# The last block's values made among the first attention scores, with the on-chip buffers of two stages laid out anew

## The chip, the cores and the metric

The kernel runs on one core of a Trainium2 chip, as one program. The metric is the time of one execution on the device in microseconds (us), and for several runs their median. The kernel before took 3134.0 us in the median of three runs (3131.89, 3134.0 and 3134.24).

## The reference

4096 nodes with 256 features each pass through two layers, both with the same adjacency matrix `adj`:

1. a graph attention network of two levels (8 heads of width 32; the weights are a softmax of leaky sums over the neighbours);
2. a transformer layer with 8 heads of width 32 and a mask.

The change concerns the second layer:

```python
qkv = layer_norm(x, g1, be1) @ w_qkv
qkv = qkv.reshape(n, 3, HEADS, HEAD_DIM)
q, k, v = (qkv[:, 0], qkv[:, 1], qkv[:, 2])
scores = jnp.einsum('nhd,mhd->hnm', q, k) * SCALE
mask = (adj != 0)[None, :, :]
scores = jnp.where(mask, scores, -jnp.inf)
attn = jax.nn.softmax(scores, axis=-1)
out = jnp.einsum('hnm,mhd->nhd', attn, v).reshape(n, DIM)
x = x + out @ w_proj + b_proj
h2 = layer_norm(x, g2, be2)
ff = jax.nn.gelu(h2 @ w1 + b1) @ w2 + b2
return x + ff
```

## The kernel before

Four stages follow each other on one core: the graph attention network (up to about 1600 us of the profile), the projections to queries, keys and values (to about 1690 us), masked attention (to about 2865 us) and the feed-forward part (to the end). The change touches the second stage and the beginning of the third, both in `unshifted_transformer`. Line numbers are those of the profile.

**The projections (L1782 to L1853).** The nodes are cut into eight blocks of 512 (`nb`). For each block PE does, in this order:

- it turns the normed rows of the next block (`Ahead.turned`, L1598; 8 transposes at L1556), and ScalarE writes them as columns `hn` (L1559);
- four tiles of keys and then queries (`i` is 1 and then 0, `c` is 0 and 1; L1810), each of 128 × 512 in fp32. ScalarE casts a tile to fp16 (L1817), and VectorE takes the rest that the cast lost (L1818). The halves lie in `u_halves`, three buffers, and SP writes them to `half_d` in DRAM (L1822);
- four tiles of values (L1829), which ScalarE copies to `v_sb` (L1836), the tile `u_v` of the profile.

An fp32 matrix multiplication shows as two passes in the profile, so a block has 16 passes at L1810 and 16 at L1829. One pool, `u_ps_q`, gives the eight banks of PSUM in turn to transposes, keys, queries and values.

The keys come back from `half_d` into two tiles `u_k` (`stack`, L1734). Of blocks 0 to 4 only half is loaded, and VectorE copies it to the other half (L1846); of blocks 5 to 7 all is loaded. Only SP's order is written by hand in this stage (L1788). On the other engines a scheduler orders the instructions by its own estimates, within what waits allow.

**Attention (L1856 to L2051).** A unit is one block of 512 queries, one group of four heads and one tile of 128 keys; there are 512 units, each of two steps `u` with two heads. A step, in `weights` (L1863 to L1882), is:

- PE: 8 score matmuls into a tile `u_ps` of 128 × 1024 (L1872), which takes two banks; the pool `u_ps_s` has three such tiles;
- ScalarE: the exponential in place (L1879);
- VectorE: the product with the mask into a tile `u_e` of 128 × 1024 in fp32 (L1881), one of ten in the pool `u_work`.

I call the result of a step an exponential and count them from 0 to 1023. Two more things use it. In `weigh` (L1898) PE multiplies it with the values into the bank `u_av`, four parts a unit; in `total` (L1912) PE sums it over the keys into the bank `u_dn`. So that PE has less to sum, GpSimd first adds the exponentials of two neighbouring units (L2026) into `u_both`, one of six tiles in the same pool `u_work`. Every eighth pair is left without this sum (`alone`), and there PE sums the exponentials themselves.

The orders of PE, ScalarE, VectorE and SP in attention are written by hand (L2005 to L2009): the loop at L2010 issues a step's scores, exponential and product, then takes three (now and then four) parts from the list `waiting`. The parts of unit `i` enter the list two units later, those of its sum four units later. VectorE's instructions that are still left of the projections can be placed between the first exponentials.

**Where the buffers lie.** A pool takes room on the left or on the right side of the on-chip memory, and gives it back when its stage ends. `pools.close()` (L1853) gives back `g_stage` and `g_rows` on the right, which hold the columns `hn`, the weights `w_qkv` (`g_adj`) and the rows of the first three blocks. On the left, `u_hv` (the halves) and `u_x` (the rows of blocks 3 to 7) are given back, and `u_work` then lies there. A new tile over an old one waits for the last instruction or DMA that used the old one. The pools of score and sum banks in PSUM lie over `u_ps_q` in the same way. `blocks` holds two tiles `u_q` for the queries of two blocks.

Of the kernel before, what the change touches and what calls it, by code (L numbers as in the profile page):

```python
# [8 lines left out]
F32 = mybir.dt.float32  # L9
# [10 lines left out]
PSUM = bass.MemoryType.PSUM  # L20
DRAM = bass.MemoryType.DRAM

P = 128
# [1544 lines left out]
class Ahead:  # L1568
# [26 lines left out]
    def normed(self, nb):  # L1595
        self.norms.normed(self.xs[nb], self.xs[nb], self.held.pop(nb))

    def turned(self, nb, c, pt):  # L1598
        if c == 0:
            self.hn[nb] = self.stage_p.tile([P, self.D // P, 512], F32, name="g_ft", tag="stage")  # L1600
        self.norms.turned(self.hn[nb], c, self.xs[nb], pt, 1)

# [31 lines left out]
def unshifted_transformer(  # L1634
# [22 lines left out]
    nc = tc.nc  # L1657
    N, D = out.shape
    DC = D // P
# [3 lines left out]
    NB = 512  # L1663
# [56 lines left out]
    with ExitStack() as scope:  # L1720
# [59 lines left out]
                load()  # L1780

        with ExitStack() as qkv:  # L1782
            hv = qkv.enter_context(tc.tile_pool(name="u_hv", bufs=3))
            ps_q = qkv.enter_context(tc.tile_pool(name="u_ps_q", bufs=8, space=PSUM))
            u_x = qkv.enter_context(tc.tile_pool(name="u_x", bufs=5))
            wq_sb = ahead.w

            qkv.enter_context(tc.manual_schedule(engines={mybir.EngineType.SP}))  # L1788
            for nb in range(3, 6):
                ahead.load(nb, u_x)  # L1790
            for nb in range(NNB):
                cols = slice(nb * NB, (nb + 1) * NB)
                hn = ahead.hn.pop(nb)
                if nb == 1:
                    for later_nb in range(6, NNB):
                        ahead.load(later_nb, u_x)
                if nb + 1 < NNB:
                    for c in range(DC):
                        ahead.turned(nb + 1, c, ps_q.tile([P, NB], F32, name="misc"))
                if 2 < nb + 2 < NNB:  # L1800
                    ahead.moments(nb + 2)
                    if nb + 3 == NNB:
                        nc.scalar.activation(rooted, ahead.held[nb + 2][:, 0, 1:2], AF.Exp)
                    ahead.normed(nb + 2)
                for i in (1, 0):
                    halves = hv.tile([P, 2, DC, NB], F16, name="u_halves")
                    for c in range(DC):
                        pq = ps_q.tile([P, NB], F32, name="misc")
                        for k in range(DC):
                            nc.tensor.matmul(  # L1810
                                pq,
                                wq_sb[k][:, i * D + c * P : i * D + (c + 1) * P],
                                hn[:, k, :],
                                start=(k == 0),
                                stop=(k == DC - 1),
                            )
                        nc.scalar.copy(halves[:, 0, c, :], pq)  # L1817
                        nc.vector.tensor_tensor(  # L1818
                            halves[:, 1, c, :], pq, halves[:, 0, c, :], op=ALU.subtract
                        )  # L1820
                    for kind in range(2):
                        nc.sync.dma_start(  # L1822
                            half_d[i, kind, :, :, cols].rearrange("c p n -> p c n"),
                            halves[:, kind],
                        )
                for t in range(TB):
                    pv = ps_q.tile([P, NB], F32, name="misc")
                    for k in range(DC):
                        nc.tensor.matmul(  # L1829
                            pv[:, :D],  # L1830
                            hn[:, k, t * P : (t + 1) * P],
                            wq_sb[k][:, 2 * D : 3 * D],
                            start=(k == 0),
                            stop=(k == DC - 1),
                        )
                    nc.scalar.copy(v_sb[:, nb * TB + t, :], pv[:, :D])  # L1836

                for b in (nb - 1,) if nb + 1 < NNB else (nb - 1, nb):
                    if b >= 0:
                        at = slice(b * NB, (b + 1) * NB)  # L1840
                        for c in range(DC):
                            late = b >= NNB - 3
                            kinds = (0, 0, 1, 1) if late else (0, None, 1, None)
                            stack(k_st[c][:, :, at], 1, kinds, at, c, HC)
                            for o in () if late else (0, 2 * O):
                                nc.vector.tensor_copy(  # L1846
                                    k_st[c][o + O : o + 2 * O, :, at], k_st[c][o : o + O, :, at]
                                )
                    if b == 0:
                        load_queries(0)  # L1850
                if 2 <= nb < 2 + NT // MC:
                    load_chunk(0, nb - 2)
        pools.close()  # L1853


        work = scope.enter_context(tc.tile_pool(name="u_work", bufs=10))  # L1856
        tail = scope.enter_context(tc.tile_pool(name="u_tail", bufs=1))
        ps_s = scope.enter_context(tc.tile_pool(name="u_ps_s", bufs=3, space=PSUM))
        ps_a = scope.enter_context(tc.tile_pool(name="u_ps_a", bufs=1, space=PSUM))
# [38 lines left out]
        def weigh(nb, c, mt, es, part):  # L1898
            if mt == 0 and part == 0:
                sums_of["av"] = ps_a.tile([P, NB], F32, name="u_av")  # L1900
            h = c * HC
            lefts = [v_sb[:, mt, (h + j) * O : (h + j + 1) * O] for j in range(HC)]
            four(sums_of["av"], lefts, es, part, mt == 0, mt == NT - 1)
            if mt == NT - 1 and part == PARTS - 1:
                num = tail.tile([P, NB], F32, name="u_num", bufs=2)
                nc.scalar.copy(num, sums_of["av"])
                nc.sync.dma_start(att_d[c, :, nb * NB : (nb + 1) * NB], num)

        def alone(mt):
            return mt // 2 % 8 == 7  # L1910
# [99 lines left out]
        for i in range(len(units) + 5):  # L2010
            for u in range(HC // 2):
                if i < len(units):
                    nb, c, mt = units[i]
                    if u == 0 and nb + 1 < NNB:
                        if c == 0 and mt == 20:
                            pacing.extend(query_steps(nb + 1))
                        if c == DC - 1 and mt % MC == 2:
                            pacing.extend(chunk_steps(nb + 1, mt // MC))
                    if u == 0 and units[i] == (NNB - 1, DC - 1, 4):
                        load_early()  # L2020
                    if u == 0:
                        pace()
                    es_of.setdefault(i, []).append(weights(*units[i], u))
                    if i % 2 == 1 and not alone(mt):
                        both = work.tile([P, 2, NB], F32, name="u_both", bufs=6)
                        nc.gpsimd.tensor_tensor(both, es_of[i - 1][u], es_of[i][u], op=ALU.add)  # L2026
                        both_of.setdefault(i, []).append(both)
                if u == 0 and 0 <= i - 2 < len(units):
                    ready(weigh, i - 2, es_of[i - 2])
                if u == 1 and i - 4 in both_of:  # L2030
                    ready(total, i - 4, both_of.pop(i - 4))
                if u == 1 and 0 <= i - 2 < len(units) and alone(units[i - 2][2]):
                    ready(total, i - 2, es_of[i - 2])
                more = (2 * i + u) % 8 == 6 and len(waiting) > 3 or len(waiting) > 5 * PARTS
                count = AFTER[i % 2 * 2 + u] + more
                for _ in range(min(count, len(waiting))):
                    waiting.pop(0)()
            for k, unit in enumerate(((NNB - 1, DC - 1, NT // 2 - 1), units[-1])):
                if i < len(units) and units[i] == unit:
                    res, att, inv = early[k]  # L2040
                    nc.gpsimd.tensor_tensor(
                        res, res, early["bp"].to_broadcast([P, TB, D]), op=ALU.add
                    )
                    nc.gpsimd.tensor_tensor(att, att, inv, op=ALU.mult)
            if i == len(units) - 1:
                nc.scalar.activation(rooted, norms.eps, AF.Sqrt)
            if i % 2 == 0 and later:
                later.pop(0)()
# [5 lines left out]
    with ExitStack() as scope:  # L2054
# [34 lines left out]
        def turned(res_n):  # L2089
            hn = ln.tile([P, DC, NB], F32, name="ln_cols")  # L2090
            for c in range(DC):
                norms.turned(hn, c, res_n, ps_m.tile([P, NB], F32, name="misc"), 2)
            return hn
# [162 lines left out]
```

## Time and profile before

| | |
|---|---|
| Median of three runs | 3134.0 us |
| Profiled execution | 3132.63 us, its span 3130.8 us |
| PE busy in the span | 3068.0 us (98%) |
| VectorE (DVE) busy | 2777.1 us (89%) |
| ScalarE (ACT) busy | 2690.3 us (86%) |
| GpSimd (POOL) busy | 1194.4 us (38%) |
| DMA queue of SP | 241.37 MB, 24.9% of 16 engines |
| L1881, mask product | 1024 of 128 × 1024, 1159.9 us in all |
| L1810 and L1829 | 128 passes each, 592 and 379 ns from start to end |
| L1817 and L1836 | 32 each, 585 and 372 ns in the middle |

The span runs from the first to the last instruction that the profiler saw; the execution's own time has 1.8 us more around it. Busy times of PE are counted to the modelled end of each pass, and passes overlap[...]. Durations of VectorE overlap as well, by the start of the next instruction. So the pace of a stage is read from starts and from whole stretches, not from the mean of one instruction. In brackets, a timeline line gives the idle time of the engine ahead of the group and what ended it. A wait for several things is put down to the last of them by the profile, and the tile named with a DMA can be another one.

### The profile page before, as it was taken

To read this page: it belongs to the slowest core of one execution; us is meant where nothing else is said; L and a number is where in the kernel's file an instruction comes from. 1 tells how busy PE (TensorE), PEld (TensorE's weight loads), DVE (VectorE), ACT (ScalarE), POOL (GpSimd) and SP (SyncE) were. 2 spreads that over 40 slices of the span, in tenths; PEclk is the share of its full clock that TensorE was granted. 3 is DMA by queue.
4 is the path that set the end of the run, shared out by engine and by line. 5 is a ranking of instruction groups with operands and counts; after the bars stand their busy time and mean duration, and the time that the engine had idled before them with its cause. 6 is when DMAs were issued, how large, how long until landed. Compare 5 with 4: busy or idle time off the path is not lost.

```text
span 3130.8 us, 139193 instructions
## 1 busy us (share of the span) xinstructions
PE 3068.0 (98%) x63976; PEld 2713.3 (87%) x63976; DVE 2777.1 (89%) x3140; ACT 2690.3 (86%) x3340; POOL 1194.4 (38%) x538
## 2 busy tenths in 40 slices
PE   6999999999999999999999999999999999999998
PEld 5899999999889999999975888888888888887766
DVE  7999999999989999999986999999999999997220
ACT  6899999999899999999965999999999999996232
POOL 3300000000330000000002998999998999997110
PEclk8999999999999999999999999999999999999999
DMA  8666555431311313121144101010101100013110
GB/s 261 219 198 207 164 184 156 150 97 30 106 44 31 93 52 97 43 63 43 47 125 142 34 21 38 21 38 28 34 21 34 31 28 28 28 41 105 63 34 22
DMA packets 213170, 250.34 MB, mean 80 GB/s; under 512 B 89120, under 2 KB 133664, under 8 KB 212576
## 3 DMA queue, kind: packets, MB, share of 16 engines
q1 hardware_dynamic: 212576, 241.37, 24.9%
q8 instruction: 502, 8.22, 1.0%
q14 instruction: 92, 0.75, 0.1%
HBM read 198.84 MB, written 42.47 MB: 77 GB/s over the span
## 4 chain that ended last, share of the span: by engine, by line
PE 50%; ACT 1%; DVE 1%; POOL 1%; issue 0%; DMA 0%; SPq 0%; DVEq 0%; ACTq 0%; POOLq 0%
PE u_ps L1872 14%; PE u_av L1890 14%; PE u_dn L1890 8%; PE misc L2135 4%; PE misc L2115 4%; PE bank L1463 3%; PE misc L1810 2%; POOL u_both L2026 1%; PE misc L2076 1%; PE misc L1829 1%; ACT t L1122 1%; PE misc L1556 0%; DVE u_e L1881 0%; DVE t L1137 0%; DVE t L1124 0%
## 5 line engine op out<-in xcount | busy, mean ns | idle before, releaser
L1463 PE MATMUL bank<-vst,t 128*128 128x132 f16 x16384 | 1455.7, 220 | 3.7 <-DVE t L1137 2.9
L2026 POOL TENSOR_TENSOR u_both<-u_e 128x1024 f32<-128x1024 f32 x448 | 1048.0, 2383 | 882.9 <-DMA u_k<-half_d 776.2
L1463 PE MATMUL bank<-vst,mask 128*128 128x132 f16 (+1 forms) x10516 | 1372.2, 206 | 0.0
L1122 ACT ACTIVATE t<-s_b,g_terms 128x1024 int8<-128x1024 f32 x1234 | 1318.6, 1148 | 21.0 <-PE bank L1463 15.2
L1463 PEld LDWEIGHTS <-t 128*128 128x128 fp8e4 x16384 | 1186.1, 96 | 15.6 <-DVE t L1137 5.4
L1881 DVE SCALAR_TENSOR_TENSOR u_e<-u_mask,u_ps 128x1024 f32<-128x1024 uint8 x1024 | 1159.9, 1214 | 9.1 <-DMA u_k<-half_d 4.5
L1879 ACT ACTIVATE u_ps<-u_ps 128x1024 f32<-128x1024 f32 x1024 | 1029.9, 1009 | 117.3 <-PE u_ps L1872 44.1
L1463 PEld LDWEIGHTS <-mask 128*128 128x128 fp8e4 x10516 | 920.4, 98 | 0.0
L1137 DVE SCALAR_TENSOR_TENSOR t<-mask,t 128x2048 int32<-128x2048 int32 x256 | 588.0, 2297 | 74.6 <-ACT t L1122 66.3
L1872 PE MATMUL u_ps<-u_q,u_k 128*32 128x512 f16 x8192 | 637.2, 382 | 6.2 <-DVE u_e L1881 3.8
L1890 PE MATMUL u_av<-u_e,u_v 128*32 128x128 f32 x16384 | 606.3, 273 | 0.0
L1124 DVE TENSOR_SCALAR t<-s_b,g_terms 128x1024 fp8e4<-128x1024 f32 x814 | 590.4, 759 | 2.6 <-DMA s_b<-s_d 2.6
L1890 PEld LDWEIGHTS u_av<-u_e,u_v 128*32 128x32 f32 x16384 | 486.4, 110 | 119.6 <-issue 0.9
L1054 POOL TENSOR_TENSOR vst<-g_adj,vst 128x528 f16<-128x528 f32 x16 | 19.9, 1241 | 725.7 <-ACT g_big L1018 681.6
L1890 PE MATMUL u_dn<-u_both,u_ones 128*32 128x128 f32 x7168 | 282.0, 273 | 2.6 <-POOL u_both L2026 2.5
L1872 PEld LDWEIGHTS <-u_k 128*32 128x32 f16 x8192 | 230.5, 96 | 37.8 <-issue 9.5
L1890 PEld LDWEIGHTS u_dn<-u_both,u_ones 128*32 128x32 f32 x7168 | 215.0, 110 | 54.6 <-POOL u_both L2026 3.7
L2122 ACT ACTIVATE u_hid<-misc,n_b 128x512 f32<-128x512 f32 x64 | 43.9, 687 | 140.2 <-PE misc L2115 140.2
L2135 PE MATMUL misc<-u_k,u_hid 128*128 128x256 f32 x512 | 111.8, 379 | 0.0
L2115 PE MATMUL misc<-ln_cols,u_k 128*128 128x512 f32 x256 | 111.3, 592 | 0.5 <-ACT ln_cols L1559 0.5
L2135 PEld LDWEIGHTS misc<-u_k,u_hid 128*128 128x128 f32 x512 | 96.7, 190 | 13.3 <-issue 0.5
L2115 PEld LDWEIGHTS misc<-ln_cols,u_k 128*128 128x128 f32 x256 | 48.6, 190 | 58.5 <-issue 56.7
(176 smaller groups left out, 1823.1 us busy)
## 6 DMA issues: line engine op xcount, KB each, us to landing
g_adj<-in_adj_dram SPq DMA_DIRECT2D x123, 512.0 KB
s_b<-s_d SPq DMA_DIRECT2D x64, 512.0 KB
mask<-mask SPq DMA_DIRECT2D x128, 256.0 KB
u_mask<-mask SPq DMA_DIRECT2D x64, 256.0 KB
mask<-stage SPq DMA_DIRECT2D x48, 256.0 KB
half_d<-u_halves SPq DMA_DIRECT2D x32, 256.0 KB
u_q<-half_d SPq DMA_DIRECT2D x32, 256.0 KB
rows<-e_x SPq DMA_DIRECT2D x31, 256.0 KB
```

The source lines that it names most:

```text
L1122: nc.scalar.activation(to.bitcast(I8), s, AF.Sign, bias=negd, scale=-1.0)
L1124: nc.vector.tensor_scalar(to, s, negd, -1.0, op0=ALU.is_ge, op1=ALU.mult, saturate=False)
L1137: nc.vector.scalar_tensor_tensor(both, m32.unsqueeze(1).to_broadcast(list(both.shape)), SIGNS, both, op0=ALU.bitwise_or, op1=ALU.bitwise_and,)
L1463: nc.tensor.matmul(to, left, right, start=k not in opened, stop=last)
L1810: nc.tensor.matmul(pq, wq_sb[k][:, i * D + c * P : i * D + (c + 1) * P], hn[:, k, :], start=(k == 0), stop=(k == DC - 1),)
L1872: nc.tensor.matmul(ps[r * O : (r + 1) * O, j, :], k_st[c][:, 2 * u + j, at : at + O], q_st[:, h, :], start=True, stop=True,)
L1879: nc.scalar.activation(ps, ps, AF.Exp, scale=SCALE)
L1881: nc.vector.scalar_tensor_tensor(e, mask, 0.0, ps, op0=ALU.not_equal, op1=ALU.mult)
L1890: nc.tensor.matmul(to[j * O : (j + 1) * O, at], lefts[j], es[j // 2][:, j % 2, at], start=first and part == 0, stop=last and part == PARTS ...
L2026: nc.gpsimd.tensor_tensor(both, es_of[i - 1][u], es_of[i][u], op=ALU.add)
L2115: nc.tensor.matmul(ph, w1_sb[:, k, f * P : (f + 1) * P], hn[:, k, :], start=(k == 0), stop=(k == DC - 1),)
L2135: nc.tensor.matmul(po[:, :D], hid[:, f, at : at + P], w2_sb[:, f, :], start=(f == 0), stop=(f == FC - 1),)
```

## The change

It has five parts.

1. **Values of the last block (`nb` 7).** The loop over values in the projections is skipped for it. A new function, `last_values(t)`, makes the four quarters in attention's loop: `t` 0, 1 and 2 after step 2, `t` 3 after step 4. Quarters 0 and 1 go to the bank that is to become `u_av`, 2 and 3 to the bank of `u_dn`, and ScalarE copies each two together to `v_sb`. The columns of block 7 (`hn_last`) and another copy of the value weights (`wv_last`, two DMAs of 128 KB by SP in block 3) lie in `spare`, a tile of the pool `blocks` that is free at that time.
2. **Banks of the projections** come from two pools: one of six banks, one of two. `bank()` takes every fourth from the small pool. In block 7 the keys take theirs from the large pool and the queries from the small one. Later the scores lie over the large pool, and the two sums over the small one.
3. **Exponentials** (`u_work`, ten tiles) lie on the right side, over `g_stage` and `g_rows`.
4. **GpSimd's sums** (`u_both`, six tiles) have a pool of their own, `u_adds`, on the left.
5. **Halves** have four buffers, not three.

In the resulting instruction lists ScalarE casts queries ahead of the values in blocks 3 to 6 as well, and two of VectorE's key copies (L1846) of block 4 stand between exponentials 0 and 1 and between 1 and 2.

```diff
-    def turned(self, nb, c, pt):
-        if c == 0:
+    def turned(self, nb, c, pt, to=None):
+        if to is not None:
+            self.hn[nb] = to
+        elif c == 0:
             self.hn[nb] = self.stage_p.tile([P, self.D // P, 512], F32, name="g_ft", tag="stage")
...
-            hv = qkv.enter_context(tc.tile_pool(name="u_hv", bufs=3))
-            ps_q = qkv.enter_context(tc.tile_pool(name="u_ps_q", bufs=8, space=PSUM))
+            hv = qkv.enter_context(tc.tile_pool(name="u_hv", bufs=4))
+            psums = [
+                qkv.enter_context(tc.tile_pool(name=f"u_ps_q{k}", bufs=n, space=PSUM))
+                for k, n in enumerate((6, 2))
+            ]
+            used = []
+
+            def bank(which=None):
+                used.append(None)
+                k = len(used) % 4 == 0 if which is None else which
+                return psums[k].tile([P, NB], F32, name="misc")
+
...
+            spare = blocks.tile([P, 4 * NB], F32, name="u_q")
+            hn_last = spare[:, : DC * NB].rearrange("p (c n) -> p c n", c=DC)
+            wv_last = spare[:, DC * NB : DC * NB + DC * D].rearrange("p (c e) -> p c e", c=DC)
...
-                        ahead.turned(nb + 1, c, ps_q.tile([P, NB], F32, name="misc"))
+                        to = hn_last if nb + 2 == NNB else None
+                        ahead.turned(nb + 1, c, bank(), to)
+                if nb == 3:
+                    for c in range(DC):
+                        nc.sync.dma_start(
+                            wv_last[:, c], ahead.w_qkv[c * P : (c + 1) * P, 2 * D : 3 * D]
+                        )
...
-                        pq = ps_q.tile([P, NB], F32, name="misc")
+                        pq = bank(1 - i if nb + 1 == NNB else None)
...
-                for t in range(TB):
-                    pv = ps_q.tile([P, NB], F32, name="misc")
+                for t in range(TB) if nb + 1 < NNB else ():
+                    pv = bank()
...
-        work = scope.enter_context(tc.tile_pool(name="u_work", bufs=10))
+        work = scope.enter_context(tc.tile_pool(name="u_work", bufs=10, side="right"))
+        adds = scope.enter_context(tc.tile_pool(name="u_adds", bufs=6))
...
+        def last_values(t):
+
+            at, name = (NNB - 1) * TB + t // 2 * 2, ("u_av", "u_dn")[t // 2]
+            if t % 2 == 0:
+                sums_of[name] = ps_a.tile([P, NB], F32, name=name)
+            to = sums_of[name]
+            for k in range(DC):
+                nc.tensor.matmul(
+                    to[:, t % 2 * D : (t % 2 + 1) * D],
+                    hn_last[:, k, t * P : (t + 1) * P],
+                    wv_last[:, k, :],
+                    start=(t % 2 == 0 and k == 0),
+                    stop=(t % 2 == 1 and k == DC - 1),
+                )
+            if t % 2 == 1:
+                nc.scalar.copy(
+                    v_sb[:, at : at + 2, :].rearrange("p t d -> p (t d)"), sums_of.pop(name)
+                )
...
                     es_of.setdefault(i, []).append(weights(*units[i], u))
+                    for t in {2: (0, 1, 2), 4: (3,)}.get(2 * i + u, ()):
+                        last_values(t)
                     if i % 2 == 1 and not alone(mt):
-                        both = work.tile([P, 2, NB], F32, name="u_both", bufs=6)
+                        both = adds.tile([P, 2, NB], F32, name="u_both")
```

## The prediction, made before the changed kernel had run

> **What bounds the kernel now.** I read the page first (which engine is full in which slice), then the busy times by stretch around the seam between the last projections and attention, then the timeline of that seam, and last the chain of what ended last. The stretches:
>
> ```profile
> 1668.00:1679.00 11.00, 11.00 (x41) 6.74 (x40) 5.32 (x8) 4.95 (x10) 0.00 (x0) 1.00 0.62 203
> 1690.00:1692.20 2.20, 0.00 (x0) 0.01 (x1) 1.29 (x2) 1.18 (x3) 0.00 (x0) 0.98 0.04 14
> 1692.20:1695.00 2.80, 2.75 (x24) 1.04 (x25) 0.00 (x0) 1.69 (x2) 0.00 (x0) 0.50 0.70 228
> 1695.00:1700.00 5.00, 1.71 (x24) 0.82 (x27) 3.50 (x4) 2.18 (x4) 0.00 (x0) 0.84 0.73 210
> 1700.00:1705.00 5.00, 4.80 (x104) 3.53 (x99) 4.09 (x4) 3.63 (x4) 4.69 (x2) 0.76 0.89 185
> 1800.00:2000.00 200.00, 200.00 (x5836) 163.55 (x5828) 200.00 (x179) 181.28 (x200) 178.80 (x77) 1.00 0.10 29
> ```
>
> After start, end and length the columns are PE, weight loads, VectorE, ScalarE and GpSimd busy, then the granted clock, the DMA share and GB/s. In the projections PE is full (11.00 of 11.00). In attention VectorE is full (200.00 of 200.00), PE too by its modelled ends. Between the two, from 1690 to 1705, nobody is full, and TensorE's clock falls to half. The change works on these 15 us only. The timeline of the seam:
>
> ```profile
> 1679.31 7.03 PE L1810 MATMUL misc<-g_ft,g_adj 128*128 128x512 f32 x16
> 1684.29 2.83 DVE L1846 COPY u_k<-u_k 32x2048 f16<-32x2048 f16 x4
> 1686.18 3.62 PE L1829 MATMUL misc<-g_adj,g_ft 128*128 128x256 f32 x16
> 1690.10 1.08 ACT L1817 CAST u_halves<-misc 128x512 f16<-128x512 f32 x2
> 1690.72 1.29 DVE L1818 TENSOR_TENSOR u_halves<-misc,u_halves 128x512 f16<-128x512 f32 x2 [3.61 <-ACT u_halves L1817]
> 1692.22 2.75 PE L1872 MATMUL u_ps<-u_q,u_k 128*32 128x512 f16 x24 [2.42 <-issue]
> 1696.50 5.75 DVE L1881 SCALAR_TENSOR_TENSOR u_e<-u_mask,u_ps 128x1024 f32<-128x1024 uint8 x5 [4.49 <-DMA u_k<-half_d]
> 1697.78 0.61 PE L1872 MATMUL u_ps<-u_q,u_k 128*32 128x512 f16 x8 [2.80 <-DVE u_e L1881]
> 1703.16 41.95 DVE L1881 SCALAR_TENSOR_TENSOR u_e<-u_mask,u_ps 128x1024 f32<-128x1024 uint8 x37 [0.91 <-ACT u_ps L1879]
> ```
>
> Read it as three waits in a row. PE finishes V of the last block at 1689.8 and waits until 1692.2: the score banks are banks of the projections, and the last two were read late, because ScalarE cast the last queries only after four V copies. VectorE then waits until 1696.5, though the first exponentials were ready at 1694.3: its output tile lies over the query halves, which a DMA is still reading. PE then waits for VectorE, with three score buffers. From exponential 5 at 1703.16 VectorE never pauses: 41.95 us for 37, **1.134 us each**. Drawn back, the unbroken stream of exponentials begins at 1703.16 − 5 × 1.134 = **1697.49**. All idle time ahead of VectorE's 1024 exponentials is 9.2 us by line, 5.4 of it in these two brackets; a later start is paid one for one.
>
> That the start carries to the end, the chain says: exponentials, then GpSimd's sums behind them, then PE with the feed-forward part without a gap.
>
> ```profile
> 2829.32 5.75 DVE u_e L1881 x5
> ...
> 2835.82 28.11 POOL u_both L2026 x12
> ...
> 2866.64 7.17 PE misc L2076 x32
> ```
>
> [...]in half-microsecond stretches the clock changes near 1692.1, 1695.5, 1698.9 and 1702.3, 3.4 us apart, half after a window with 2.2 us of idle time[...]. [...]Here the last query half was issued from 1692.04 to 1692.40, and VectorE was released at 1696.50, 4.1 us later, beside 16 other issues; I use 4.1. [...]So three score tiles of 1024 columns plus two sums take all eight, and each must lie over a projection bank.
>
> **The change part by part.**
>
> *V of the last block leaves the projections.* PE loses 16 passes × 0.213 = 3.4 us there, so scores may start at 1686.18. ScalarE loses four copies × 0.37. The query casts, with a fourth buffer of halves, now stand ahead of the exponentials with no V copies before them. A tile's four passes take 1.72: keys were cast at 1681.23 and 1682.95, so queries at 1684.67 and 1686.39, the last until 1686.97, and VectorE's subtraction follows from 1687.01 to 1687.70.
>
> *Banks in two pools of six and two.* Last keys in the six, which the scores take; last queries in the two, which V and the sums take. The first score waits only for the keys' subtraction (done at 1684.25). One bank in four goes to the small pool, so each is reused after eight takings as before: nothing on PE in the projections.
>
> *Exponentials on the other side.* By the instruction lists the first one now waits for ScalarE alone, not for six DMA queues. Scores 0 to 2 take 0.43 each on PE (1706.70 to 1707.13 in the steady part); the first is readable at 1686.18 + 0.62 = 1686.80. ScalarE is free at 1686.97: exponential 0 from 1687.0 to 1688.0, VectorE from **1688.03**.
>
> *Two key copies move into the stream.* The lists put two of the four L1846 copies after exponentials 0 and 1; before, they ran in idle time. 2.83 / 4 = 0.71 each, 1.42 in all, with the next exponential already waiting. Their DMAs landed before 1684.29, so no wait comes with them. Stream start: 1688.03 + 1.42 = **1689.45**.
>
> *V comes back among the scores.* Three quarters (6 matmuls × 0.427 = 2.56) after score 2, the last (0.85) after score 4. It waits for the last query subtraction, 1687.70, and ends near 1690.3. Score 3 follows until 1690.7, is exponentiated from 1690.9 to 1691.9 and is due on VectorE at 1689.45 + 3 × 1.134 = 1692.85: 0.9 us to spare. Score 5 stands behind V's last quarter and three parts of weighing (0.64); it needs exponential 2 gone (1692.85) and is due at 1695.1; near 1693.6 ScalarE can take it. Two copies of 512 columns, 0.58 each as for u_num, stand in ScalarE's queue, which needs 1.01 of 1.134 per step. Cost: nothing, covered by VectorE's stream and by PE's missing weighings in the first four steps (4 × 0.65); uncovered it would be up to 3.4.
>
> *Sums in a pool of their own.* GpSimd's first sum still waits for all eight queues, so for the last query half: issued until 1688.1, landed near 1692.2; exponential 2 is done at 1692.85. Nothing. Behind it only exponential 10 needs that buffer, at 1700.8.
>
> *Two loads of V's weights (128 KB each) on SP* in block 3: two issues near 0.43 = 0.9 us, where SP waits up to 7.2 us for ScalarE; the mask and half transfers behind them have a block of slack. Nothing; uncovered 0.9.
>
> *Unknown: the clock in the new seam.* PE's idle pieces are now 0.2 to 0.5 us, no window is mostly idle. Value taken: full clock; other end: half for two windows, V at 5.1 instead of 2.6, which costs 2.6. *Unknown: the rate at the new addresses.* Exponentials lie between 1159 and 1222 ns over all ten old buffers, so I take no effect; bound ±0.1% of 1161 us, ±1.2.
>
> **Sum.** 1697.49 − 1689.45 = **8.0 us**. The profiled execution took 3132.6 (span 3130.8 and 1.8 around it), so 3124.6; the median of the runs shown is 1.4 above it: 3134.0 − 8.0 = **3126.0**.
>
> A check from PE's side, in case PE is the full engine: V's 3.4 us stay on it, and what goes is idle time, 2.42 + 2.80 + 0.52 and about 0.5 up to 1706.7, plus lost clock: 1.3 in the first half window, 1.7 in the second. That is 9.2, less some 1.6 of new small gaps: 7.6. Both views agree.
>
> **Rivals.**
> *Slow clock or a late first score* (chance 0.14). If the score banks are given back only with the whole pool, scores wait for 1687.7 and 1.2 us go; if the clock halves, 2.6. 3127.2 to 3129.8, about 3128.6. For it: this seam did halve twice. Against: the gaps are a tenth of those.
> *The exponentials are still held by a DMA* (0.06). If the right side or GpSimd's ring ties the stream to the last query half, it starts near 1692.2 to 1693.5 and 4 to 5 us remain: 3129.5. Against: the listed waits name none.
> *Slower: the new place slows the stream* (0.06). Exponentials are written by VectorE and read by GpSimd and PE 1024 times. One per cent is 11.6 us and gives 3137.6; from 0.7% (7.8 ns in 1134) the gain is gone. For it: such leverage. Against: the ten old buffers show no dependence on address.
> *Forecast* 0.74.
>
> **How the numbers follow.** A measurement of this kernel can tell about 0.2%, 6.3 us, from no change: faster means below 3127.7. The forecast spans some 3124 to 3127.7 (copies out of the way 1.0 better; a stall near 2820 us, where the clock drops too, may fall 1 us either way). The first two rivals lie within 0.2%. So faster 0.74, same 0.20, slower 0.06. The range 3123.5 to 3129.5 leaves out the slow rival, half the second and a tail below.
>
> **What would show it.** First exponential on VectorE near 1688, two key copies after exponentials 0 and 1, no idle bracket over 0.3 behind them; PE without a bracket over 0.5 between projections and scores; clock 1.00 throughout; the feed-forward part starts 8 us earlier. Wrong if VectorE's first bracket names a DMA, if the exponentials differ from 1.134 on average, or if blocks 0 to 6 no longer take 11.19 us each.

## The result

The changed kernel took 3125.84 us in the median (16 runs, 3124.63 to 3127.15), the kernel before 3132.68 us beside it (16 runs, 3129.5 to 3134.24). The ratio is 0.9979, with a 95% interval of 0.9971 to 0.9986: faster by 6.84 us (by the interval 4.4 to 9.1). The profiled execution took 3125.56 us, its span is 3123.7 us (before 3132.63 and 3130.8).

First the stretches of the changed kernel, with the columns of the prediction:

```profile
1668.00:1679.00 11.00, 11.00 (x41) 6.74 (x40) 5.50 (x8) 5.19 (x10) 0.00 (x0) 1.00 0.55 186
1686.00:1700.00 14.00, 13.29 (x225) 8.47 (x225) 13.25 (x15) 11.73 (x14) 6.66 (x3) 1.00 0.73 189
1800.00:2000.00 200.00, 200.00 (x5824) 163.27 (x5820) 199.91 (x180) 181.17 (x199) 180.46 (x78) 1.00 0.10 29
```

The stages on both sides are as full as before. The seam is filled: VectorE is busy for 13.25 of 14.00 us, PE for 13.29, and the clock stays at 1.00. The timeline of the seam shows who stands where:

```profile
1686.35 1.48 PE L1894 MATMUL u_ps<-u_q,u_k 128*32 128x512 f16 x24
...
1687.07 0.69 DVE L1839 TENSOR_TENSOR u_halves<-misc,u_halves 128x512 f16<-128x512 f32 x1 [0.31 <-ACT u_halves L1838]
...
1687.82 1.99 PE L1938 MATMUL u_av<-u_q 128*128 128x256 f32 x8
1688.05 1.22 DVE L1903 SCALAR_TENSOR_TENSOR u_e<-u_mask,u_ps 128x1024 f32<-128x1024 uint8 x1 [0.29 <-ACT u_ps L1901]
...
1689.31 0.68 DVE L1867 COPY u_k<-u_k 32x2048 f16<-32x2048 f16 x1
...
1690.02 1.22 DVE L1903 SCALAR_TENSOR_TENSOR u_e<-u_mask,u_ps 128x1024 f32<-128x1024 uint8 x1
...
1691.27 0.69 DVE L1867 COPY u_k<-u_k 32x2048 f16<-32x2048 f16 x1
...
1691.99 23.84 DVE L1903 SCALAR_TENSOR_TENSOR u_e<-u_mask,u_ps 128x1024 f32<-128x1024 uint8 x21
```

All three waits of before are gone: PE goes from the last queries to the scores without a bracket, exponential 0 waits 0.29 us for ScalarE and for no DMA, and from exponential 2 (1691.99) VectorE doesn't pause. Drawn back, the stream starts at 1691.99 − 2 × 1.134 = **1689.72**, where it was 1697.49. The chain of waits has the order of before:

```profile
2821.96 5.75 DVE u_e L1903 x5
2828.41 28.16 POOL u_both L2069 x12
2859.28 7.17 PE misc L2119 x32
```

The feed-forward part starts at 2859.28 instead of 2866.64.

### The profile page after: what moved, and what is told of

It is laid out like the page before. It is cut to its first block, busy times and chain, and to the rows that moved or that the text cites. A ratio compares the mean times of both kernels' runs of the same rounds, so it can differ in the third digit from the quotient of the medians.

```text
span 3123.7 us, 139197 instructions
## 1 busy us (share of the span) xinstructions
PE 3066.3 (98%) x63976; PEld 2711.5 (87%) x63976; DVE 2777.6 (89%) x3140; ACT 2691.6 (86%) x3338; POOL 1196.2 (38%) x538
## 4 chain that ended last, share of the span: by engine, by line
PE 49%; POOL 1%; DVE 1%; ACT 1%; issue 0%; DMA 0%; SPq 0%; DVEq 0%; ACTq 0%; POOLq 0%
PE u_ps L1894 14%; PE u_av L1912 14%; PE u_dn L1912 8%; PE misc L2178 4%; PE misc L2158 4%; PE bank L1463 3%; PE misc L1831 2%; POOL u_both L2069 1%; PE misc L2119 1%; ACT t L1122 1%; PE misc L1850 1%; DVE u_e L1903 0%; PE misc L1556 0%; DVE t L1137 0%; DVE t L1124 0%
```

## The experiments

Each edit is made to the changed kernel, unless said otherwise. From run to run the projections end up to 2.4 us earlier or later, so a stream start is only compared within its own trace: I measure it from ScalarE's first cast of a last key tile. It is 1697.49 − 1681.23 = 16.26 us before and 1689.72 − 1681.30 = **8.42 us** in the changed kernel. From the same cast to the end of the span, every run through e8 differs from the changed kernel by what its stream start differs, within 0.9 us.

| run | median, us (range) | ratio to before [95%] | against the changed kernel's 3125.84 | stream start after the cast |
|---|---|---|---|---|
| before | 3132.68 (3129.5–3134.24) | | +6.84 | 16.26 |
| changed | 3125.84 (3124.63–3127.15) | 0.9979 [0.9971, 0.9986] | | 8.42 |
| e1, exponentials on the left | 3128.89 (3127.93–3130.7) | 0.9989 [0.9981, 0.9998] | +3.05 | 12.85 |
| e2, before with the new place | 3129.55 (3128.53–3130.61) | 0.9992 [0.9984, 1.0] | +3.71 | 13.11 |
| e3, values first | 3128.32 (3127.13–3130.62) | 0.9988 [0.9982, 0.9995] | +2.48 | 11.67 |
| e4, last keys whole | 3125.23 (3124.41–3127.0) | 0.9979 [0.9971, 0.9987] | −0.61 | 8.04 |
| e5, one pool of banks | 3127.32 (3125.87–3128.88) | 0.9984 [0.9977, 0.999] | +1.48 | 9.77 |
| e6, three half buffers | 3133.34 (3132.1–3135.09) | 1.0003 [0.9994, 1.0011] | +7.50 | 17.39 |
| e7, values twice | 3129.36 (3128.4–3130.95) | 0.999 [0.9982, 0.9999] | +3.52 | 11.50 |
| e8, no values | 3125.87 (3125.11–3127.19) | 0.998 [0.9972, 0.9987] | +0.03 | 8.42 |
| e4 again | 3125.41 (3124.59–3126.4) | 0.9979 [0.9971, 0.9988] | −0.43 | |
| e9, pairs 8 and 10 | 3125.99 (3124.92–3127.64) | 0.9981 [0.9972, 0.999] | +0.15 | |
| e10, pair 4 | 3121.96 (3121.16–3122.66) | 0.9969 [0.9957, 0.9981] | −3.88 | |
| e11, pairs 2 and 4 | 3121.45 (3120.9–3123.92) | 0.997 [0.9959, 0.9981] | −4.39 | |

The kernel before took 3132.23 us beside e1 to e4, 3132.5 beside e5 to e8 and 3131.81 beside the others, and 3132.68 beside the changed kernel. These differ by up to 0.9 us, so the column against the changed kernel can't tell smaller differences from nothing; the stream start, within one trace, tells them better.

My theory was the prediction's: three waits in a row go, and each part of the change is needed for that. The rivals: that V among the scores makes PE the full engine, and that the new place of the exponentials slows the stream.

**e1: exponentials back on the left, over the halves.**

```diff
-        work = scope.enter_context(tc.tile_pool(name="u_work", bufs=10, side="right"))
-        adds = scope.enter_context(tc.tile_pool(name="u_adds", bufs=6))
+        work = scope.enter_context(tc.tile_pool(name="u_work", bufs=10))
...
-                        both = adds.tile([P, 2, NB], F32, name="u_both")
+                        both = work.tile([P, 2, NB], F32, name="u_both", bufs=6)
```

> The changed kernel, but exponentials and GpSimd's sums lie in one pool over the halves again. Theory (VectorE's stream sets the end, one for one with its start): exponential 0 waits for the write of the last query half, issued until 1688.2 and landed 4.1 later, so it starts near 1692.2 instead of 1688.05, and the stream near 1692.2 to 1693.6 instead of 1689.7: 2.5 to 3.9 us slower than the changed kernel. Rival A (the place does nothing, the early scores are all): same as the changed kernel. Rival B (the place is all): as slow as the kernel before, 6.8 slower.

3.05 us slower. VectorE in the timeline of e1:

```profile
1690.78 5.74 DVE L1902 SCALAR_TENSOR_TENSOR u_e<-u_mask,u_ps 128x1024 f32<-128x1024 uint8 x5 [2.65 <-DMA half_d<-u_halves]
1698.75 13.66 DVE L1902 SCALAR_TENSOR_TENSOR u_e<-u_mask,u_ps 128x1024 f32<-128x1024 uint8 x12 [2.23 <-ACT u_ps L1900]
```

The old wait is back under its name: 2.65 us for the DMA that still reads the halves. It ended 3.7 us after SP had issued the last half (1687.08), near the 4.1 us that the prediction used. A second wait, of 2.23 us ahead of exponential 5, stands behind it: late exponentials hold the score buffers, and PE's next scores come late. PE stands idle for 2.45 us ahead of score 3 and for 0.52 ahead of score 4, and what follows takes longer on it: V's last quarter, which stands ahead of score 5, 2.08 us instead of 1.13, and the 24 passes of weighing behind it 1.49 instead of 0.86. Both key copies ran in the first gap, so the loss is less than the sum of the brackets.

**e2: the kernel before with this part alone.**

```diff
-        work = scope.enter_context(tc.tile_pool(name="u_work", bufs=10))
+        work = scope.enter_context(tc.tile_pool(name="u_work", bufs=10, side="right"))
+        adds = scope.enter_context(tc.tile_pool(name="u_adds", bufs=6))
...
-                        both = work.tile([P, 2, NB], F32, name="u_both", bufs=6)
+                        both = adds.tile([P, 2, NB], F32, name="u_both")
```

> The kernel before with only the places changed (exponentials right, sums left). Theory: scores still begin at 1692.2, exponential 0 is ready at 1694.3 and taken then, not at 1696.5; 2.0 to 2.5 us faster than before. Rival B (the place is all): 6.8 us faster than before. Rival C (the new place slows each exponential): VectorE's start-to-start rises above 1.134 and the time rises with it.

2.68 us faster than the kernel before beside it. In the timeline of e2 the DMA wait is gone, and the stream runs without a gap, but it begins late:

```profile
1694.56 18.18 DVE L1882 SCALAR_TENSOR_TENSOR u_e<-u_mask,u_ps 128x1024 f32<-128x1024 uint8 x16 [2.33 <-ACT u_ps L1880]
```

The bracket now names ScalarE: PE's scores are still late, behind the last banks. So the place takes 3.15 us off the stream start (16.26 to 13.11) and all the rest without the place 3.41 us (16.26 to 12.85, e1). Together they take 7.84, 1.3 more than the sum: each alone leaves the other's wait in place.

**e3: the last block's values back ahead of the scores**, the other parts kept.

```diff
-                for t in range(TB) if nb + 1 < NNB else ():
-                    pv = bank()
+                for t in range(TB):
+                    pv = bank(0 if nb + 1 == NNB else None)
...
-                    for t in {2: (0, 1, 2), 4: (3,)}.get(2 * i + u, ()):
-                        last_values(t)
```

> The changed kernel, but the last block's values are made in the projections again (banks, places and four halves stay). Theory: scores begin at 1689.8, exponential 0 near 1691.5, 1.8 us later than the stream of the changed kernel (3.2 if the two key copies still lie in the stream): 1.8 to 3.2 us slower than the changed kernel. Rival PE (PE is the full engine of attention, so where V is made is all the same): within 0.7 of the changed kernel.

2.48 us slower, where PE alone has 16 × 0.216 = 3.5 us more to do ahead of the scores: V's passes start 0.216 us apart in the traces of before and of the changed kernel, where the prediction took 0.213. The timeline of e3:

```profile
1691.62 5.74 DVE L1903 SCALAR_TENSOR_TENSOR u_e<-u_mask,u_ps 128x1024 f32<-128x1024 uint8 x5 [2.89 <-ACT u_ps L1901]
...
1698.18 14.79 DVE L1903 SCALAR_TENSOR_TENSOR u_e<-u_mask,u_ps 128x1024 f32<-128x1024 uint8 x13 [0.82 <-ACT u_ps L1901]
```

Counted from the cast, exponential 0 is 4.0 us later than in the changed kernel (1691.62 − 1680.84 against 1688.05 − 1681.30): V's 3.5, and 0.46 in which the scores wait for ScalarE's last V copy. Both key copies were done in the gap ahead, which gives 1.4 us back, and the bracket of 0.82 is new. That makes 3.4 for a stream start that is 3.25 later.

**e4: the last keys whole**, so that no key copy stands in the stream: of block 4 too all is loaded.

```diff
-                            late = b >= NNB - 3
+                            late = b >= NNB - 4
```

> The changed kernel with the keys of block 4 loaded whole (four more loads on SP, four key copies fewer on VectorE), so that no key copy lies in the stream. Theory: the two copies cost 1.4 us of VectorE, but without them exponential 3, held up by V on PE, comes late: 0.5 us faster than the changed kernel, with an idle bracket near 0.9 before exponential 3. Rival (one for one): 1.4 faster. Rival PE: no difference.

0.61 us faster by the medians, and 0.43 when e4 ran again, which they can't tell from nothing: against the kernel before beside it, e4 gained 7.00 and 6.40 us, the changed kernel 6.84. By the stream start it gains 0.38. In the timeline of e4 two new brackets stand in the stream:

```profile
1691.83 2.35 DVE L1903 SCALAR_TENSOR_TENSOR u_e<-u_mask,u_ps 128x1024 f32<-128x1024 uint8 x2 [0.78 <-ACT u_ps L1901]
1694.53 18.36 DVE L1903 SCALAR_TENSOR_TENSOR u_e<-u_mask,u_ps 128x1024 f32<-128x1024 uint8 x16 [0.35 <-ACT u_ps L1901]
```

Leaving the copies out takes 2 × 0.7 us from the stream, and these waits, ahead of exponentials 3 and 5, give most of it back. Both are for ScalarE; at exponential 3 it waits for score 3 in its turn, and that stands right behind three quarters of V on PE (1687.33 to 1690.12). So by the stream start the copies cost 0.4 us, not 1.42.

**e5: one pool of eight banks** for the projections.

```diff
-                for k, n in enumerate((6, 2))
+                for k, n in enumerate((8,))
...
-                k = len(used) % 4 == 0 if which is None else which
+                k = 0
```

> The changed kernel with the projections' banks in one pool of eight again. The first score tile then lies over the banks of the last queries and waits for VectorE's subtraction there (done at 1687.76), 1.4 us later than now; one key copy goes ahead of exponential 0 in that time. Theory: stream 0.7 us later, so 0.7 slower than the changed kernel. Rival (the two pools are needed for the early scores): as slow as with the values first, 2.5 slower. Rival (pools do nothing): same.

1.48 us slower. PE in the timeline of e5:

```profile
1689.18 1.48 PE L1894 MATMUL u_ps<-u_q,u_k 128*32 128x512 f16 x24 [1.40 <-DVE u_halves L1839]
```

The scores wait for the last query subtraction, as the prediction's rival of a late first score had it (1.2 us). I had expected half of that here, since one key copy moves into the gap; it did, but 0.64 us of a new bracket ahead of exponential 5 took that back. Whether the scores wait because they lie over just these banks, or because the pool is given back as a whole, this run doesn't tell.

**e6: three half buffers**, as before.

```diff
-            hv = qkv.enter_context(tc.tile_pool(name="u_hv", bufs=4))
+            hv = qkv.enter_context(tc.tile_pool(name="u_hv", bufs=3))
```

> The changed kernel with three buffers of halves. By its instruction lists ScalarE casts the last queries behind exponential 2, and VectorE subtracts them behind its exponential 2 (near 1694.2); V waits for that bank, and score 3 stands behind V on PE. Theory: exponential 3 on VectorE at 1698.4 instead of 1692.9, 5.5 us slower than the changed kernel, and up to 8.5 slower if PE's idle time there halves its clock. Rival (a buffer that only one block lacks costs a DMA wait of 1 us or nothing): 0 to 1 slower.

7.50 us slower: without the fourth buffer nothing is left of the gain. The timeline of e6:

```profile
1689.51 1.10 ACT L1838 CAST u_halves<-misc 128x512 f16<-128x512 f32 x2
...
1692.89 1.28 DVE L1839 TENSOR_TENSOR u_halves<-misc,u_halves 128x512 f16<-128x512 f32 x2
1694.28 3.75 PE L1938 MATMUL u_av<-u_q 128*128 128x256 f32 x8 [6.68 <-issue]
...
1701.43 2.35 DVE L1903 SCALAR_TENSOR_TENSOR u_e<-u_mask,u_ps 128x1024 f32<-128x1024 uint8 x2 [7.26 <-ACT u_ps L1901]
```

With three buffers the scheduler puts the last query casts behind exponentials 0 to 2 on ScalarE and their subtractions behind exponential 2 on VectorE. V needs the banks of those queries, so PE waits 6.68 us, and V then runs at a granted clock of 0.50 (1693 to 1699; 3.75 us for what took 1.99). The next scores stand behind V in PE's queue: VectorE waits 7.26 us. Whether ScalarE could have cast earlier with three buffers, under another order, no run tells.

**e7: V's passes in attention twice.**

```diff
-            for k in range(DC):
+            for n in range(2 * DC):
+                k = n % DC
...
-                    start=(t % 2 == 0 and k == 0),
-                    stop=(t % 2 == 1 and k == DC - 1),
+                    start=(t % 2 == 0 and n == 0),
+                    stop=(t % 2 == 1 and n == 2 * DC - 1),
```

> The changed kernel with each of the 8 multiplications of the last values issued twice into the same sum (the values of the last block come out doubled). PE's work in the seam grows by 3.4 us. Theory (VectorE is the full engine, PE has about 0.9 us to spare ahead of exponential 3): 2.6 us slower than the changed kernel, with idle brackets of that sum on VectorE. Rival PE (full): 3.4 slower, and the same difference in the other direction where the values are left out. Rival (all is covered): same.

3.52 us slower by the median, which is near the number of the rival PE (3.4), and 3.08 by the stream start, which lies between the two. The timeline of e7 tells more:

```profile
1695.62 2.35 DVE L1903 SCALAR_TENSOR_TENSOR u_e<-u_mask,u_ps 128x1024 f32<-128x1024 uint8 x2 [1.69 <-ACT u_ps L1901]
1699.19 9.14 DVE L1903 SCALAR_TENSOR_TENSOR u_e<-u_mask,u_ps 128x1024 f32<-128x1024 uint8 x8 [1.22 <-ACT u_ps L1901]
```

Three quarters more are 12 × 0.216 = 2.59 us, of which 1.69 arrive at exponential 3: 0.9 us were spare there, as forecast. The last quarter more is 0.86; 1.22 arrive at exponential 5, 0.4 more than itself, so the 2.6 of the theory was too low. From e7 alone the rival could not be refused; e8 decides between them, because the rival must gain there what it loses here.

**e8: no passes of V at all**; ScalarE copies the first block's values in their place.

```diff
-            if t % 2 == 0:
-                sums_of[name] = ps_a.tile([P, NB], F32, name=name)
-            to = sums_of[name]
-            for k in range(DC):
-                nc.tensor.matmul(
...
-                )
...
-                    v_sb[:, at : at + 2, :].rearrange("p t d -> p (t d)"), sums_of.pop(name)
+                    v_sb[:, at : at + 2, :].rearrange("p t d -> p (t d)"),
+                    v_sb[:, at % 4 : at % 4 + 2, :].rearrange("p t d -> p (t d)"),
```

> The changed kernel without the 8 multiplications of the last values: ScalarE copies the values of the first block in their place, so the last block's values are wrong. Theory (V is hidden behind VectorE's stream): 0 to 0.3 faster than the changed kernel, unless the idle time on PE halves its clock there, then up to 1.5 slower. Rival PE (full engine): 3.4 faster.

0.03 us slower, and the same stream start: 3.5 us of PE work taken away change nothing. V among the scores is hidden whole, and the rival that PE sets the pace falls. In PE's timeline of e8 two brackets stand where V was:

```profile
1689.75 0.61 PE L1894 MATMUL u_ps<-u_q,u_k 128*32 128x512 f16 x8 [1.50 <-DVE u_e L1903]
1691.71 0.86 PE L1894 MATMUL u_ps<-u_q,u_k 128*32 128x512 f16 x8 [1.35 <-DVE u_e L1903]
```

Its stretches, cut near where the clock changes:

```profile
1688.70:1692.10 3.40, 1.00 (x16) 0.50 (x19) 3.31 (x4) 3.00 (x4) 0.00 (x0) 0.98 0.74 228
1692.10:1695.50 3.40, 3.40 (x55) 2.33 (x51) 3.37 (x4) 2.25 (x3) 1.73 (x1) 0.52 0.88 210
```

PE is busy for 1.00 of 3.40 us, and in the next 3.40 its clock is 0.52. VectorE is as full as in the changed kernel in both (3.31 and 3.37 us, there 3.27 and 3.40): even this slow clock is hidden here.

**The late wait (e9, e4 again, e10, e11).** After the seam, what VectorE still loses in attention lies near 2815 us. The timeline of the changed kernel:

```profile
2814.52 1.22 DVE L1903 SCALAR_TENSOR_TENSOR u_e<-u_mask,u_ps 128x1024 f32<-128x1024 uint8 x1 [1.08 <-POOL u_both L2069]
...
2817.36 1.22 DVE L1903 SCALAR_TENSOR_TENSOR u_e<-u_mask,u_ps 128x1024 f32<-128x1024 uint8 x1 [1.61 <-ACT u_ps L1901]
...
2819.49 35.35 DVE L1903 SCALAR_TENSOR_TENSOR u_e<-u_mask,u_ps 128x1024 f32<-128x1024 uint8 x31 [0.91 <-ACT u_ps L1901]
```

The kernel before has the same three (1.05, 2.23 and 0.47), with a mean clock of 0.83 from 2820 to 2830. GpSimd has two additions and two products of 2.4 us each among its sums there (L2084 and L2087, made early for the first rows of the feed-forward part). If GpSimd is late, PE can sum some pairs without it.

```diff
-        def alone(mt):
-            return mt // 2 % 8 == 7
+        def alone(nb, c, mt):
+            last = (nb, c) == (NNB - 1, DC - 1)
+            return mt // 2 % 8 == 7 or last and mt // 2 in (8, 10)
...
-                    if i % 2 == 1 and not alone(mt):
+                    if i % 2 == 1 and not alone(*units[i]):
...
-                if u == 1 and 0 <= i - 2 < len(units) and alone(units[i - 2][2]):
+                if u == 1 and 0 <= i - 2 < len(units) and alone(*units[i - 2]):
```

This and e4's edit make e9. It ran beside e4 again.

> The version with the last keys copied whole (e4), and in the last group of scores two pairs of tiles are added up on the PE alone instead of on GpSimd first, near where VectorE is held up late in the stream of exponentials (brackets of 1.08, 1.61 and 0.91 us between 2813 and 2829 in the changed kernel, 3.6 together). Theory, that GpSimd is the cause there (four products of some 2.4 us each stand among its sums, and it is nearly full): some 9 us less work for GpSimd, so most of the 3.6 us goes; 1.5 to 3 us faster than the changed kernel, of which 0.6 is e4's. Rival, that the PE is as full there as GpSimd: two pairs without a sum cost the PE some 1.7 us, and the run is 0.5 to 1.2 us slower than the changed kernel.

> The same kernel as e4 beside e9_best on one chip: 0.6 us faster than the changed kernel, as before, and the measure for e9_best.

e9 missed: it gains nothing, 0.58 us slower than e4 beside it in the median and 0.3 from the cast to the end of the span. But the pairs were chosen badly. In the timeline of e4 again PE waits twice for sums:

```profile
2813.72 0.74 PE L1912 MATMUL u_dn<-u_both,u_ones 128*32 128x128 f32 x18 [1.89 <-POOL u_both L2069]
2820.73 0.52 PE L1912 MATMUL u_dn<-u_both,u_ones 128*32 128x128 f32 x10 [1.14 <-POOL u_both L2069]
```

Counted from 2780.92, where the last group's sums begin on GpSimd, these are the sums of pairs 5 and 6. Pairs 8 and 10 come after both, and in e9 the wait of 1.89 us stands as before. The next two runs take pairs ahead of them, `== 4` (e10) and `in (2, 4)` (e11) in place of `in (8, 10)`:

> e4 with one pair of tiles (pair 4 of the last group of scores) left without GpSimd's sum, so 4.7 us less for GpSimd ahead of the sums of pairs 5 and 6, which PE waited for at 2813.7 (1.89 us) and 2820.7 (1.14 us) in the run of e4. Theory, that these two waits make VectorE's late brackets (3.3 us there): they go, PE pays 0.86 us for the pair, VectorE's brackets fall below 1.5 us, and the run is 1 to 2.5 us faster than e4. Rival, that PE is full there with or without the wait, as the run with pairs 8 and 10 left out suggested: VectorE's brackets stay near 3 us, named by ScalarE, and the run takes e4's time or up to 0.9 us more.

> As e10, with pair 2 left out too. Theory: GpSimd was already early enough with one pair left out, so a second one only costs PE its 0.86 us, some of it in idle time: 0 to 0.9 us slower than e10. Rival, that GpSimd is still late with one pair left out: up to 1.5 us faster than e10.

e10 is 3.45 us faster than e4 again (3.8 from the cast to the end of the span), more than I gave it: all three brackets go (1.08, 1.16 and 1.10 in e4 again), PE no longer waits for a sum, and PE's cost for the pair isn't seen. VectorE at the end of attention in e10:

```profile
2794.25 0.25 DVE L1974 RECIPROCAL u_inv<-u_dens 128x16 f32<-128x16 f32 x1
2794.40 56.60 DVE L1903 SCALAR_TENSOR_TENSOR u_e<-u_mask,u_ps 128x1024 f32<-128x1024 uint8 x50
```

The last fifty exponentials follow each other without a bracket. So GpSimd was the cause of the late wait, and e9 failed by its place and not by its reason. e11 takes the same time as e10 (0.5 us less in the median, within the scatter, and the same to 0.03 us from the cast to the end): with one pair left out GpSimd is early enough. e10 is the simpler version that beats both kernels, 9.85 us faster than the kernel before beside it.

## Why the prediction was right

The forecast was 3126.0 us by way of 8.0 us; measured were 3125.84 and 6.84. By its steps:

- **The banks and the first score.** Forecast 1686.18, seen 1686.35. The rival of a late first score was priced at 1.2 us; e5 made it happen and lost 1.48.
- **The half buffers and the casts.** The last query was to be cast from 1686.39 and subtracted until 1687.70; it was 1686.45 and 1687.76. The prediction named the fourth buffer in half a sentence and gave it no price. e6 shows that without it, and the order of the casts that comes with it, nothing of the gain is left.
- **The place of the exponentials.** Exponential 0 was to reach VectorE at 1688.03, waiting for ScalarE alone; it was 1688.05. e1 brings the DMA wait back. The rival of a slower stream falls: 64 exponentials in the changed kernel's later stream take 72.42 us, 1.13 each, as before. The rival of a stream still held by a DMA falls with the 0.29 us bracket.
- **Two key copies in the stream** cost 2 × 0.71 there, as the trace has it. But the prediction took this for the price of having them there. Without them V is late next, and e4 gains only 0.4 by the stream start.
- **V among the scores** was to cost nothing, with 0.9 us to spare at score 3. e8 (nothing gained without it) and e7 (2.59 us more, 1.69 of them seen at exponential 3) show both numbers. Uncovered it was put at up to 3.4; e3 paid 2.48.
- **Sums in a pool of their own.** GpSimd's first sum begins at 1693.35, for a forecast not before 1692.85, and the exponentials behind it show no bracket. It was not tested apart: e1 and e2 move the sums together with the exponentials.
- **V's weights and the banks inside the projections** were to cost nothing. Blocks 0 to 6 still start 11.19 to 11.20 us apart on PE, as before.
- **The clock** stays at 1.00, the value taken.

Where 8.0 became 6.84: the stream starts 7.77 us earlier instead of 8.0, at 1689.72 for 1689.45. Exponential 0 is only 0.02 late, but from it to exponential 2 pass 3.94 us instead of 3.69: ahead of a copy an exponential takes its full 1.22 us, not 1.134, and there are gaps of 0.03 around the copies. The term that was carried one for one to the end shrinks a little on its way: 7.83 us at the group of exponentials that starts at 1850.70 (before 1858.53), 7.42 at the one at 2721.66 (before 2729.08), 7.36 at the start of the feed-forward part, 7.1 in the spans. The 0.4 lost within attention is no slower rate: between these two points three groups of 64 exponentials take 72.68 to 72.75 us in the changed kernel, the others 72.50 to 72.58. The same three are long in e5 and e8 and none is in e4 again, which has the new place too, so the place isn't the reason; the cause stays open. The remaining 0.3 between 7.1 and the medians' 6.84 is less than the interval.

That the predicted median came within 0.2 us is partly luck: the gain was put 1.16 too high, and the base 1.32 too high as well, since it rests on the three runs shown, whose median was 3134.0, where the runs beside the changed kernel had 3132.68.

The check from PE's side came to nearly the same sum, 7.6, without being the mechanism: taking V's 3.5 us from PE gains nothing (e8), since VectorE sets the pace at the seam.

## What to carry to other kernels

When several waits stand in a row at a seam between two stages, cost the start of the next stage's full engine, and ask of each part of a change what is late next without it: here the place alone gave 2.7 us, all the rest without it 3.3, both 6.8, and without one small buffer nothing. Look at the number of buffers of a pool as part of the instruction order, because the scheduler decides with it who comes first. And follow a late engine's wait back to the piece of work that was due, then relieve the engine ahead of that piece: pair 4 gained 3.5 us where pairs 8 and 10 gained nothing.

## What was not expected of the hardware

- **The clock fell after shorter gaps than in the kernel before.** There the stretches with a clock of 0.50 and 0.51 (1692.10 and 1698.90, 3.40 us each) came after brackets of 2.42 and 2.80 us on PE. In e8 no bracket is longer than 1.50 us, but PE was busy for only 1.00 of the 3.40 us from 1688.70, and in the next 3.40 the clock was 0.52. A longer gap did not bring it down at once: in e6 PE did nothing from 1687.60 to 1694.28, the clock was 1.00 up to 1693.00, and 0.50 from there to 1699.00. So the longest gap doesn't tell when the clock falls; what does, these runs don't settle. In the changed kernel V fills the stretch that is nearly empty in e8 (3.33 of 3.40 us busy from 1688.70 to 1692.10), and the clock was 1.00 there and in the next 3.40 us: V among the scores went with a clock that stayed up.
- **Equal stages don't start at equal times.** The projections' last keys were cast between 1680.23 and 1682.67 in the traces of before, changed and e1 to e8, though nothing ahead of block 3 differs among the changed kernel's versions. The programs of e10 and e11 are the same up to the last group of scores, and yet exponential 0 begins at 1689.05 and 1687.72; their spans, 3120.4 and 3119.1 us, differ by the same 1.3. A mark within the trace takes that out.
